# Attention over shared keys with the keys on the partitions, in a one-core graph-transformer kernel

## The chip, the core and the metric

The kernel runs on one core of a Trainium2 chip. The metric is the device time of one execution in microseconds; the median of several executions stands for a kernel. A profile of one further execution gives busy times, waits and the order of the work.

## The reference

The program is two layers of a graph network with 625 nodes of 1024 features. Each layer adds a graph convolution, a linear attention and a feed-forward part to its input. The change is inside the feed-forward part of the second layer, which itself begins with a softmax attention of four heads of 256 features. All heads share one set of keys and values:

```python
nx = _rmsnorm(X, g1)
Q = (nx @ Wq.T).reshape(B, S, H, dk).transpose(0, 2, 1, 3)   # 4 heads of 256
Kc = nx @ Wkc.T                                              # 625 x 256, one for all heads
Vc = nx @ Wvc.T
scores = jnp.einsum('bhsd,btd->bhst', Q, Kc) * scale         # scale = 1/16
attn = jax.nn.softmax(scores, axis=-1)
out = jnp.einsum('bhst,btd->bhsd', attn, Vc)
out = out.transpose(0, 2, 1, 3).reshape(B, S, d) @ Wo.T
X = X + out
```

Behind it come a shared expert and two of eight routed experts for each row. The weights that make Q and Kc are normal with a deviation of 0.02; everything is float32.

## The kernel before

The 625 nodes are five tiles of 125 (`NT`, `P`), padded to 626 columns where they lie in the free dimension (`NP`), which are two halves of 313 (`HN`)[...]. Up to the expert blocks the order on every engine is written by hand: `do(prep, pe, after, after2)` issues a piece of TensorE work (`pe`), issues its `after` just ahead of the next piece's `pe`, and its `after2` just ahead of the one after that. So what an engine does is in the order of the `do` calls, and an engine works strictly in that order; semaphores hold an instruction until its inputs are there and its output's buffer is free.

All double PSUM tiles (`ps2`, two banks) come from one set of three buffers, used in turn; single ones (`ps1`) from two. SBUF tiles come from pools with tags: `big` has two buffers of eight rows of 640 floats per partition, `w` six of one megabyte for weights.

In the attention, `nxT` holds the normalised rows with features on partitions. From it come the keys `kcT` (features on partitions, 2 x 626), the values `vc` (nodes on partitions) and, head by head, the queries `qT` (features on partitions, two buffers). The stage's loop over heads takes, per tile `t` of 125 queries:

- `score` (L1208): scores with queries on the partitions and 626 keys in the free dimension; then on VectorE the largest score of a row (L1219, L1220), on ScalarE the exponential with that as a bias and with the row's sum (L1223), and on VectorE the sum's reciprocal and the division of the row (L1228 to L1230);
- `turn_scores`: the five 125 x 125 transposes of the row block on TensorE (L1239), copied by VectorE and ScalarE (L1243, L1244) into `pT`, which has the keys on partitions;
- `attend`: for each half of a head's 256 features, the product of values and `pT` over the five key tiles, copied into `aT`.

The loop puts the next head's queries (`ahead`, in halves) and the last head's two `attend`s between the scores, so that TensorE has work while a row block is made. Behind the loop stand the loads of Wo, the last `attend`s, and `project(t)`, the product with Wo (tile `pX`), whose `prep` scales the residual on VectorE.

The program contains the whole computation twice. `attempt(False)` runs the first graph attention without subtracting a row's largest score and tests whether its denominators stayed in a range; two columns of ones and zeros (`inside`) are summed over the partitions by a product with ones in `ranks`, turned into the number `again`, and read by the engines at the end. If `again` is above zero, `attempt(True)` computes everything anew with the shift. In both, the attention described here subtracts the maximum.

Of the kernel before, what the change touches and what calls it, by code (L numbers as in the profile page):

```python
# [8 lines left out]
FP = mybir.dt.float32  # L9
# [3 lines left out]
AF = mybir.ActivationFunctionType  # L13
ALU = mybir.AluOpType
AX = mybir.AxisListType
# [3 lines left out]
N = 625  # L19
NT = 5  # L20
P = 125
NP = 626
HN = 313
# [5 lines left out]
D = 1024  # L29
KC = D // 128  # L30
NE = 8
NB = 17
NB_MIN = 10
FAR = -1.0e30
LIMIT = 60.0
LEAST, MOST = 1.0e-22, 1.0e25
# [13 lines left out]
def attempt(ctx: ExitStack, tc: tile.TileContext, w: dict, out: bass.AP, shifted: bool):  # L50

    nc = tc.nc

    const = ctx.enter_context(tc.tile_pool(name="const", bufs=1))
# [4 lines left out]
    def ps1(name):  # L59
        pool, n = psums[-1]  # L60
        return pool.tile([128, 512], FP, tag="ps1", name=name, bufs=n)

    def ps2(name):
        return psums[-1][0].tile([128, 2, 512], FP, tag="ps2", name=name, bufs=3)


    ident = const.tile([128, 128], FP, name="ident")
# [5 lines left out]
    ones = const.tile([128, 128], FP, name="ones")  # L73
# [3 lines left out]
    nc.vector.memset(blockmask[0:64, 0:64], 1.0)  # L77
    nc.vector.memset(blockmask[64:128, 64:128], 1.0)

    inside = const.tile([128, 2], FP, name="inside")  # L80
    nc.vector.memset(inside, 1.0)

    def test(col, src, n, pool):
# [11 lines left out]
    def copy(dst, src):  # L95

        turn[0] ^= 1
        if turn[0]:
            nc.vector.tensor_copy(dst, src)
        else:  # L100
            nc.scalar.activation(dst, src, AF.Copy)  # L101
# [21 lines left out]
    def group(dst, pairs):  # L123

        for i, (lhsT, rhs) in enumerate(pairs):
            nc.tensor.matmul(dst, lhsT=lhsT, rhs=rhs, start=(i == 0), stop=(i == len(pairs) - 1))  # L126

    def feat(name, pairs):

        p = ps2(name)  # L130
        for h in range(2):
            group(p[:, h, :HN], [(a, b[:, h * HN:(h + 1) * HN]) for a, b in pairs])
        return p[:, :, :HN]

    def halves(ap):
        return ap.rearrange("p (h n) -> p h n", h=2)

    def nodes(t):
        return slice(t * P, (t + 1) * P)
# [54 lines left out]
    big = graph.enter_context(tc.tile_pool(name="big", bufs=2))  # L194
# [7 lines left out]
    do = Stream()  # L202
    hold = {}
# [7 lines left out]
    class LinearAttention:  # L211
# [82 lines left out]
        def query(self, m):  # L294
            if m % 4 == 0:
                self.wq = Half(wpool, w[self.names[0]], m // 4)
            wq = self.wq

            def pe():
                hold["pq"] = feat("pq", [(wq(k, m % 4 * 128, 128), self.xnT[:, k, :]) for k in range(KC)])  # L300

            def after():
                pq = hold["pq"]
                qe = mix.tile([128, NP], FP, tag="qe", name="qe", bufs=1)
                nc.scalar.activation(halves(qe), pq, AF.Exp, bias=self.bq[:, m:m + 1])
                qf = mix.tile([128, NP], FP, tag="qf", name="qf", bufs=2)
                nc.scalar.activation(halves(qf), pq, AF.Relu, bias=self.bq[:, m:m + 1])  # L307
                nc.vector.scalar_tensor_tensor(qf, qe, 1.0, qf, op0=ALU.min, op1=ALU.add)
                hold["qf", m] = qf

            do(None, pe, after)
            self.work(8.5)
# [18 lines left out]
    with ExitStack() as st0:  # L331
# [9 lines left out]
        with ExitStack() as edges:  # L341
            pool = edges.enter_context(tc.tile_pool(name="l0e", bufs=1))
# [33 lines left out]
            up = pool.tile([128, EN], FP, name="up")  # L376
# [161 lines left out]
            ring = big.tile([128, 10, 940], BF, tag="big", name="ring", padded_shape=[128, 10, 1024])  # L538
# [9 lines left out]
            def score(dst, m, n, p):  # L548

                nc.vector.scalar_tensor_tensor(m, m, 0.2, m, op0=ALU.mult, op1=ALU.max)  # L550
                nc.vector.tensor_tensor(m, m, att[0:p].unsqueeze(1).to_broadcast([p, n, 256]), op=ALU.mult)
                nc.vector.tensor_reduce(dst, m.rearrange("p t (h e) -> p t h e", h=4), AX.X, ALU.add)
                if not shifted:
                    nc.vector.tensor_scalar(dst, dst, LIMIT, None, op0=ALU.min)
                    nc.scalar.activation(dst, dst, AF.Exp)
# [478 lines left out]
    for k in range(KC):  # L1034
# [3 lines left out]
        def pe():  # L1038
            hold["pa"] = feat("pa", [(xnh[k // 4][:, s, k % 4 * 128:k % 4 * 128 + 128], CT[:, s, :])
                                     for s in range(NT)])  # L1040

        def after(k=k):
            copy(halves(meanT[k // 4][:, k % 4, :]), hold["pa"])
# [3 lines left out]
    for m in range(KC):  # L1047
# [3 lines left out]
        a = m % 4  # L1051
# [30 lines left out]
    pool = attn.enter_context(tc.tile_pool(name="attn", bufs=1, reuse_waits="tile"))  # L1082
# [119 lines left out]
        value(t)  # L1202

    aT = bigT("aT")
    pT = big.tile([128, NT, D], FP, tag="big", name="pT")[:P, :, 0:NP]
    nc.gpsimd.memset(pT[:, :, N:NP], 0.0)

    def score(head, t):  # L1208
        q = qT[head % 2]

        def pe():
            psc = hold["psc", t] = ps2("psc")
            for h in range(2):
                group(psc[:P, h, :HN], [(q[:, a, nodes(t)], kcT[:, a, h * HN:(h + 1) * HN]) for a in range(2)])

        def after():
            psc = hold.pop(("psc", t))[:P, :, :HN]
            mx = pool.tile([P, 1], FP, tag="mx", name="mx", bufs=2)
            nc.vector.tensor_reduce(mx, psc, AX.XY, ALU.max)  # L1219
            nc.vector.tensor_scalar(mx, mx, -1.0 / 16.0, None, op0=ALU.mult)  # L1220
            pr = pool.tile([P, NP], FP, tag="pr", name="pr", bufs=3)
            den = pool.tile([P, 1], FP, tag="den", name="den", bufs=3)
            nc.scalar.activation(halves(pr), psc, AF.Exp, bias=mx, scale=1.0 / 16.0, accum_out=den)  # L1223
            hold["pr", t] = pr, den

        def after2():
            pr, den = hold["pr", t]
            nc.vector.tensor_tensor(den, den, pr[:, N:NP], op=ALU.subtract)  # L1228
            nc.vector.reciprocal(den, den)
            nc.vector.tensor_scalar(pr, pr, den, None, op0=ALU.mult)  # L1230

        do(None, pe, after, after2)

    def turn_scores(t):
        def pe():
            pr, _ = hold.pop(("pr", t))
            pp = hold["pp"] = [ps1("ppT").rearrange("p (c n) -> p c n", c=4) for i in range(2)]
            for s in range(NT):
                nc.tensor.transpose(pp[s // 4][:P, s % 4, :P], pr[:, nodes(s)], ident[:P, :P])  # L1239

        def after():
            pp = hold["pp"]
            nc.vector.tensor_copy(pT[:, 0:4, nodes(t)], pp[0][:P, :, :P])  # L1243
            nc.scalar.activation(pT[:, 4, nodes(t)], pp[1][:P, 0, :P], AF.Copy)  # L1244

        do(None, pe, after)

    def attend(head, a):
        def pe():
            hold["po", a] = feat("po", [(vc[:, s, a * 128:(a + 1) * 128], pT[:, s, :]) for s in range(NT)])  # L1250

        do(None, pe, lambda: copy(halves(aT[:, 2 * head + a, :]), hold["po", a]))

    for head in range(4):
        ahead = [query(head + 1, a) for a in range(2)] if head < 3 else [lambda h: None] * 2
        score(head, 0)
        score(head, 1)
        if head:
            attend(head - 1, 0)
            attend(head - 1, 1)  # L1260
        turn_scores(0)
        score(head, 2)
        turn_scores(1)
        score(head, 3)
        ahead[0](0)
        ahead[0](1)
        turn_scores(2)
        score(head, 4)
        turn_scores(3)
        ahead[1](0)  # L1270
        ahead[1](1)
        turn_scores(4)
    wo = [Half(wpool, w["Wo"], c) for c in range(2)]
    attend(3, 0)
    attend(3, 1)

    attn.close()
    pool = ctx.enter_context(tc.tile_pool(name="exp", bufs=1, reuse_waits="tile"))
# [160 lines left out]
    def ranks():  # L1439
        hold["prt"] = ps1("prt")  # L1440
        group(hold["prt"][:P, 0:NT * NE], [(before, flat)])
        group(hold["prt"][:P, NT * NE:2 * NT * NE], [(ones[:P, :P], flat)])
        group(hold["prt"][:P, 2 * NT * NE:2 * NT * NE + 2], [(ones[:, :P], inside)])

    do(None, ranks)
    ptot = hold["prt"][:, NT * NE:2 * NT * NE]
# [24 lines left out]
    for i in range(2):  # L1471
# [22 lines left out]
    exp_f = pool.tile([P, NB], FP, name="exp_f")  # L1494
    nc.vector.tensor_reduce(exp_f, blk, AX.X, ALU.add)
    meta = pool.tile([P, NB + 2], I32, name="meta")
    outside = pool.tile([P, 1], FP, name="outside")
    nc.vector.tensor_scalar(outside, hold["prt"][:P, 2 * NT * NE:2 * NT * NE + 1], -1.0, 256.0,
                            op0=ALU.mult, op1=ALU.add)
    nc.vector.tensor_tensor(meta[:, NB + 1:NB + 2], outside, hold["prt"][:P, 2 * NT * NE + 1:2 * NT * NE + 2],  # L1500
                            op=ALU.subtract)
    nc.vector.tensor_scalar(meta[:, 0:NB], exp_f, float(NE - 1), None, op0=ALU.min)
    nc.vector.tensor_copy(meta[:, NB:NB + 1], ends[3][:, NE - 1:NE])
    hidden(3)
# [71 lines left out]
    rest(NB_MIN)  # L1576
    again = None
    if not shifted:
        again = nc.values_load(meta[0:1, NB + 1:NB + 2], min_val=0, max_val=256,
                               skip_runtime_bounds_check_because="256 less two sums of up to 128 ones and zeros")  # L1580


    with tc.manual_schedule(engines={mybir.EngineType.PE, mybir.EngineType.DVE, mybir.EngineType.Pool}):
# [121 lines left out]
```

## Time and profile before

| what | value |
|---|---|
| three executions, us | 2294.43, 2296.43, 2296.47 |
| median, us | 2296.43 |
| profiled execution, its own time, us | 2290.41 |
| its span from first to last instruction, us | 2288.7 |
| mean granted clock of TensorE | 0.978 |
| attention stage, us from the start | 1309.7 to 1464.8 |
| projection with Wo to the first hidden layer, us | 1464.8 to 1536.9 |
| expert blocks, us | 1684 to 2211 |

PE is TensorE's matmuls, PEld its weight loads, DVE VectorE, ACT ScalarE, POOL GpSimd, SPq the queue that issues most transfers. A line of the timeline gives the start and the length in microseconds, engine, source line, operation, output tile and input tiles, shapes and a count; in brackets stands the idle time before it and what ended it. Matmuls are pipelined: the length of one runs to its end, and what it costs in a row of them is the distance from start to start. L126 is the helper that issues most matmuls, so they are told apart by their output tiles: `psc` scores, `ppT` transposes, `po` values times weights, `pq` queries, `pX` the projection. A float32 matmul of the program shows as two in the trace, a transpose as one.

### The profile page before, as it was taken

What the parts mean: (1) busy time and instruction counts of PE and PEld (TensorE: products, weight loads), DVE (VectorE), ACT (ScalarE), POOL (GpSimd) and SP (SyncE); (2) the same over time, 40 slices, a digit from 0 to 9 for tenths busy, and PEclk for the clock granted to TensorE, in tenths of its full rate; (3) what the DMA queues carried; (4) which work ended last, traced back from release to release, by engine and by line L of the source; (5) the groups of instructions that cost most, each with busy time, mean ns of one, the idle gap of its engine ahead of it and who ended that gap; (6) DMA issues with size and microseconds to landing.
All of it is one profiled execution on the core that took longest, in us unless ns stands there. A gap on an engine that the chain in (4) does not pass through costs nothing. (4 is left out here: it accounts for less than half of the span.)

```text
span 2288.7 us, 17693 instructions
## 1 busy us (share of the span) xinstructions
PE 2170.3 (95%) x7018; PEld 1228.9 (54%) x7018; DVE 734.7 (32%) x1342; ACT 196.1 (9%) x363; POOL 346.0 (15%) x351
## 2 busy tenths in 40 slices
PE   8988888987899999999999999999999999999998
PEld 6655554444445767754444777556754444444443
DVE  5868668655422640000111133232111111111112
ACT  2000010012200100000000011110000000000000
POOL 1667766300000220010000000010000000000010
PEclk9998998989999999999999999999999999999999
DMA  9352252530122110233003111030269898898643
GB/s 302 96 174 63 68 186 79 133 105 1 37 83 74 46 46 0 74 138 110 0 0 118 57 38 37 10 109 1 92 249 338 318 332 305 303 332 319 254 149 94
DMA packets 145852, 301.66 MB, mean 132 GB/s; under 512 B 12370, under 2 KB 22436, under 8 KB 145754
## 3 DMA queue, kind: packets, MB, share of 16 engines
q1 hardware_dynamic: 123412, 243.18, 29.6%
q0 software_dynamic: 17664, 47.47, 7.0%
q10 hardware_dynamic: 4678, 9.72, 1.4%
q8 instruction: 59, 0.97, 0.2%
q14 instruction: 39, 0.32, 0.0%
HBM read 277.49 MB, written 22.84 MB: 131 GB/s over the span
## 5 line engine op out<-in xcount | busy, mean ns | idle before, releaser
L126 PE MATMUL pu<-w,xgT 128*128 128x512 f32 x768 | 333.9, 593 | 1.9 <-DVE xgT L1086 1.9
L126 PEld LDWEIGHTS pu<-w,xgT 128*128 128x128 f32 x768 | 144.0, 190 | 174.8 <-issue 172.0
L126 PE MATMUL pyb<-w,hb 128*128 128x512 f32 x384 | 174.3, 598 | 2.5 <-ACT yb L101 2.1
L126 PE MATMUL pq<-xnT,w 128*128 128x313 f32 x512 | 143.0, 439 | 15.1 <-ACT qf L307 11.6
L126 PE MATMUL pv<-w,xnT 128*125 128x512 f32 x320 | 143.4, 602 | 3.7 <-issue 3.7
L126 PE MATMUL pk<-w,xnT 128*125 128x512 f32 x320 | 141.4, 595 | 4.7 <-DVE x L888 4.7
L126 PE MATMUL p<-tT,w 128*128 128x313 f32 x512 | 136.3, 428 | 0.4 <-DVE tT L1086 0.4
L126 PEld LDWEIGHTS pq<-xnT,w 128*128 128x128 f32 x512 | 99.6, 196 | 56.9 <-ACT qf L307 13.5
L126 PEld LDWEIGHTS pyb<-w,hb 128*128 128x128 f32 x384 | 69.8, 189 | 90.9 <-issue 74.9
L1539 DVE TENSOR_TENSOR su<-pu,su 128x512 f32<-128x512 f32 x24 | 16.6, 691 | 314.6 <-ACT su L1538 314.6
L126 PEld LDWEIGHTS p<-tT,w 128*128 128x128 f32 x512 | 96.8, 190 | 37.9 <-issue 1.2
L126 PEld LDWEIGHTS pk<-w,xnT 128*125 128x125 f32 x320 | 59.7, 189 | 78.9 <-issue 72.2
L126 PEld LDWEIGHTS pv<-w,xnT 128*125 128x125 f32 x320 | 60.4, 191 | 76.7 <-issue 75.9
L582 POOL DMA_INDIRECT table<-es,at x79 | 85.9, 1088 | 59.9 <-issue 27.2
L1522 POOL DMA_INDIRECT xg<-rows_d,slots x12 | 11.4, 947 | 524.7 <-PE pxg L1529 449.0
L568 POOL DMA_INDIRECT ga<-xl_d,si x79 | 81.1, 1027 | 32.1 <-issue 29.1
L568 POOL DMA_INDIRECT gb<-xr_d,di x79 | 79.6, 1008 | 24.1 <-issue 23.5
L706 PE MATMUL px<-w,oT 128*125 128x512 f32 x160 | 76.7, 639 | 4.1 <-DVE oT L326 2.3
L126 PE MATMUL px<-w,hT 128*125 128x512 f32 x160 | 70.6, 594 | 0.0
L126 PE MATMUL px<-w,oT 128*125 128x512 f32 x160 | 70.3, 592 | 0.0
L126 PE MATMUL ph<-meanT,w 128*128 128x313 f32 x256 | 70.1, 426 | 0.0
L126 PE MATMUL ph<-xnT,w 128*128 128x313 f32 x256 | 70.0, 427 | 0.0
(352 smaller groups left out, 2550.9 us busy)
## 6 DMA issues: line engine op xcount, KB each, us to landing
w<-in_eW_dram SPq DMA_DIRECT2D x144, 1024.0 KB
w<-in_L_Wk_dram SPq DMA_DIRECT2D x8, 1024.0 KB
w<-in_L_Wv_dram SPq DMA_DIRECT2D x8, 1024.0 KB
w<-in_L_Wq_dram SPq DMA_DIRECT2D x8, 1024.0 KB
w<-in_L_Wo_dram SPq DMA_DIRECT2D x8, 1024.0 KB
w<-in_W_self_dram SPq DMA_DIRECT2D x8, 1024.0 KB
w<-in_W_neigh_dram SPq DMA_DIRECT2D x8, 1024.0 KB
w<-in_sW_dram SPq DMA_DIRECT2D x8, 1024.0 KB
```

The source lines that it names most:

```text
L126: nc.tensor.matmul(dst, lhsT=lhsT, rhs=rhs, start=(i == 0), stop=(i == len(pairs) - 1))
L568: nc.gpsimd.indirect_dma_start(out=dst[0:p, j, :], out_offset=None, in_=src[:, :], in_offset=bass.IndirectOffsetOnAxis(ap=ix[0:p, lo + j:l ...
L582: nc.gpsimd.indirect_dma_start(out=table[:, :], out_offset=bass.IndirectOffsetOnAxis(ap=at[0:p, lo + j:lo + j + 1], axis=0), in_=es[0:p, l ...
L706: nc.tensor.matmul(hold["px", t][:P, c, :], lhsT=oT[:, k, nodes(t)], rhs=wo[c](k), start=(k == 0), stop=False)
L1522: nc.gpsimd.indirect_dma_start(out=xg, out_offset=None, in_=rows_d[:, :], in_offset=bass.IndirectOffsetOnAxis(ap=slots[:, b:b + 1], axis=0))
L1539: nc.vector.tensor_tensor(su, pu[:, 0, :], su, op=ALU.mult)
```

## The change

In `attempt(False)` the attention is a new function; the old one is kept, word for word, as `shifted_attention` for `attempt(True)`.

- The scores are made with the keys on the partitions: `kcT` is now the stationary and the query the moving operand. A tile `s` is 125 keys by 626 queries.
- No maximum is taken. VectorE copies the scores from PSUM with a minimum against 16 x 60, straight into one of eight slots of `ring` (in the buffer of tag `big` that `pT` had), and ScalarE takes the exponential in place. The slot is the moving operand of the values' product as it stands, so the transposes and their copies go.
- The denominators: VectorE adds a head's five tiles, a product with a matrix of ones sums over the partitions and lays the sums of all queries on all 128 partitions, and VectorE takes the reciprocal of 128 x 626.
- `attend` no longer copies its result; VectorE multiplies it by the reciprocals on its way from PSUM to `aT` (`divide`).
- One row of each head's reciprocals is kept by ScalarE (`recs`) and tested at the end against a range, into a third column of `inside`; `again` counts from 384 in place of 256.
- The order in the loop: the last head's denominators stand behind the first score of a head, and its two `attend`s behind the second and third. The last head's stand behind the loop: `attend`, denominators, `attend`, both divisions. The loads of Wo are called behind them.

```diff
+    def attention():
+        ring = big.tile([128, 8, 640], FP, tag="big", name="ring")
+        recs = pool.tile([128, NP], FP, tag="pr", name="recs", bufs=3)
+        nc.gpsimd.memset(recs, 1.0)
+
+        def pT(head, s):
+            return ring[:P, (NT * head + s) % 8, 0:NP]
+
+        def score(head, s):
+            q = qT[head % 2]
+
+            def pe():
+                psc = hold["psc", s] = ps2("psc")
+                for h in range(2):
+                    group(psc[:P, h, :HN], [(kcT[:, a, nodes(s)], q[:, a, h * HN:(h + 1) * HN]) for a in range(2)])
+
+            def after():
+                p = pT(head, s)
+                nc.vector.tensor_scalar(halves(p), hold.pop(("psc", s))[:P, :, :HN], 16.0 * LIMIT, None, op0=ALU.min)
+                nc.scalar.activation(p, p, AF.Exp, scale=1.0 / 16.0)
+
+            def after2():
+                if s == 1:
+                    hold["den", head] = pool.tile([P, NP], FP, tag="xs", name="den", bufs=2, padded_shape=[P, D])
+                    nc.vector.tensor_tensor(hold["den", head], pT(head, 0), pT(head, 1), op=ALU.add)
+                elif s:
+                    nc.vector.tensor_tensor(hold["den", head], hold["den", head], pT(head, s), op=ALU.add)
+
+            do(None, pe, after, after2)
+
+        def denominators(head):
+            def pe():
+                hold["pden"] = feat("pden", [(ones[:P, :], hold.pop(("den", head)))])
+
+            def after():
+                rec = hold["rec"] = pool.tile([128, NP], FP, tag="pr", name="rec", bufs=3)
+                nc.vector.reciprocal(halves(rec), hold["pden"])
+                nc.scalar.activation(recs[32 * head:32 * head + 1, :], rec[0:1, :], AF.Copy)
+
+            do(None, pe, after)
+
+        def attend(head, a):
+            do(None, lambda: hold.update({("po", a): feat("po", [(vc[:, s, a * 128:(a + 1) * 128], pT(head, s))
+                                                                 for s in range(NT)])}),
+               None if head == 3 else lambda: divide(head, a))
+
+        def divide(head, a):
+            nc.vector.tensor_tensor(halves(aT[:, 2 * head + a, :]), hold["po", a], halves(hold["rec"]), op=ALU.mult)
+
+        for head in range(4):
+            ahead = [query(head + 1, a) for a in range(2)] if head < 3 else [lambda h: None] * 2
+            score(head, 0)
+            if head:
+                denominators(head - 1)
+            score(head, 1)
+            if head:
+                attend(head - 1, 0)
+            score(head, 2)
+            if head:
+                attend(head - 1, 1)
+            score(head, 3)
+            ahead[0](0)
+            ahead[0](1)
+            score(head, 4)
+            ahead[1](0)
+            ahead[1](1)
+        do()
+        attend(3, 0)
+        denominators(3)
+        attend(3, 1)
+        for a in range(2):
+            divide(3, a)
+
+        c = pool.tile([128, NP], FP, tag="pr", name="c", bufs=3)
+        nc.vector.tensor_scalar(c, recs, 1.0 / MOST, 1.0 / LEAST, op0=ALU.max, op1=ALU.min)
+        nc.vector.tensor_tensor(c, c, recs, op=ALU.is_equal)
+        nc.vector.tensor_reduce(inside[:, 2:3], c, AX.X, ALU.min)
+
+    (shifted_attention if shifted else attention)()
     wo = [Half(wpool, w["Wo"], c) for c in range(2)]
-    attend(3, 0)
-    attend(3, 1)
...
-        group(hold["prt"][:P, 2 * NT * NE:2 * NT * NE + 2], [(ones[:, :P], inside)])
+        group(hold["prt"][:P, 2 * NT * NE:2 * NT * NE + 3], [(ones[:, :P], inside)])
...
-    outside = pool.tile([P, 1], FP, name="outside")
-    nc.vector.tensor_scalar(outside, hold["prt"][:P, 2 * NT * NE:2 * NT * NE + 1], -1.0, 256.0,
-                            op0=ALU.mult, op1=ALU.add)
-    nc.vector.tensor_tensor(meta[:, NB + 1:NB + 2], outside, hold["prt"][:P, 2 * NT * NE + 1:2 * NT * NE + 2],
-                            op=ALU.subtract)
+    within = pool.tile([P, 1], FP, name="within")
+    nc.vector.tensor_reduce(within, hold["prt"][:P, 2 * NT * NE:2 * NT * NE + 3], AX.X, ALU.add)
+    nc.vector.tensor_scalar(meta[:, NB + 1:NB + 2], within, -1.0, 384.0, op0=ALU.mult, op1=ALU.add)
```

More of the change, by code (lines that the diff above doesn't have):

```diff
@@ L78, in attempt @@
     nc.vector.memset(blockmask[64:128, 64:128], 1.0)
-    inside = const.tile([128, 2], FP, name="inside")
+    inside = const.tile([128, 3], FP, name="inside")
     nc.vector.memset(inside, 1.0)
@@ L1204, in attempt @@
     aT = bigT("aT")
[L1205 to L1272, printed above, removed]
+    def shifted_attention():
+        pT = big.tile([128, NT, D], FP, tag="big", name="pT")[:P, :, 0:NP]
+        nc.gpsimd.memset(pT[:, :, N:NP], 0.0)
+        def score(head, t):
+            q = qT[head % 2]
+            def pe():
+                psc = hold["psc", t] = ps2("psc")
+                for h in range(2):
+                    group(psc[:P, h, :HN], [(q[:, a, nodes(t)], kcT[:, a, h * HN:(h + 1) * HN]) for a in range(2)])
+            def after():
+                psc = hold.pop(("psc", t))[:P, :, :HN]
+                mx = pool.tile([P, 1], FP, tag="mx", name="mx", bufs=2)
+                nc.vector.tensor_reduce(mx, psc, AX.XY, ALU.max)
+                nc.vector.tensor_scalar(mx, mx, -1.0 / 16.0, None, op0=ALU.mult)
+                pr = pool.tile([P, NP], FP, tag="pr", name="pr", bufs=3)
+                den = pool.tile([P, 1], FP, tag="den", name="den", bufs=3)
+                nc.scalar.activation(halves(pr), psc, AF.Exp, bias=mx, scale=1.0 / 16.0, accum_out=den)
+                hold["pr", t] = pr, den
+            def after2():
+                pr, den = hold["pr", t]
+                nc.vector.tensor_tensor(den, den, pr[:, N:NP], op=ALU.subtract)
+                nc.vector.reciprocal(den, den)
+                nc.vector.tensor_scalar(pr, pr, den, None, op0=ALU.mult)
+            do(None, pe, after, after2)
+        def turn_scores(t):
+            def pe():
+                pr, _ = hold.pop(("pr", t))
+                pp = hold["pp"] = [ps1("ppT").rearrange("p (c n) -> p c n", c=4) for i in range(2)]
+                for s in range(NT):
+                    nc.tensor.transpose(pp[s // 4][:P, s % 4, :P], pr[:, nodes(s)], ident[:P, :P])
+            def after():
+                pp = hold["pp"]
+                nc.vector.tensor_copy(pT[:, 0:4, nodes(t)], pp[0][:P, :, :P])
+                nc.scalar.activation(pT[:, 4, nodes(t)], pp[1][:P, 0, :P], AF.Copy)
+            do(None, pe, after)
+        def attend(head, a):
+            def pe():
+                hold["po", a] = feat("po", [(vc[:, s, a * 128:(a + 1) * 128], pT[:, s, :]) for s in range(NT)])
+            do(None, pe, lambda: copy(halves(aT[:, 2 * head + a, :]), hold["po", a]))
+        for head in range(4):
[5 more added lines that the diff above has]
+                attend(head - 1, 1)
+            turn_scores(0)
+            score(head, 2)
+            turn_scores(1)
+            score(head, 3)
+            ahead[0](0)
+            ahead[0](1)
+            turn_scores(2)
+            score(head, 4)
+            turn_scores(3)
+            ahead[1](0)
+            ahead[1](1)
+            turn_scores(4)
+        attend(3, 0)
+        attend(3, 1)
@@ new lines, in attention, with pe, after, after2 @@
+    def attention():
[5 more added lines that the diff above has]
+        def score(head, s):
+            q = qT[head % 2]
+            def pe():
+                psc = hold["psc", s] = ps2("psc")
+                for h in range(2):
+                    group(psc[:P, h, :HN], [(kcT[:, a, nodes(s)], q[:, a, h * HN:(h + 1) * HN]) for a in range(2)])
+            def after():
+                p = pT(head, s)
+                nc.vector.tensor_scalar(halves(p), hold.pop(("psc", s))[:P, :, :HN], 16.0 * LIMIT, None, op0=ALU.min)
+                nc.scalar.activation(p, p, AF.Exp, scale=1.0 / 16.0)
+            def after2():
+                if s == 1:
[3 more added lines that the diff above has]
+                    nc.vector.tensor_tensor(hold["den", head], hold["den", head], pT(head, s), op=ALU.add)
+            do(None, pe, after, after2)
+        def denominators(head):
+            def pe():
+                hold["pden"] = feat("pden", [(ones[:P, :], hold.pop(("den", head)))])
+            def after():
+                rec = hold["rec"] = pool.tile([128, NP], FP, tag="pr", name="rec", bufs=3)
+                nc.vector.reciprocal(halves(rec), hold["pden"])
+                nc.scalar.activation(recs[32 * head:32 * head + 1, :], rec[0:1, :], AF.Copy)
+            do(None, pe, after)
+        def attend(head, a):
+            do(None, lambda: hold.update({("po", a): feat("po", [(vc[:, s, a * 128:(a + 1) * 128], pT(head, s))
[3 more added lines that the diff above has]
+            nc.vector.tensor_tensor(halves(aT[:, 2 * head + a, :]), hold["po", a], halves(hold["rec"]), op=ALU.mult)
+        for head in range(4):
+            ahead = [query(head + 1, a) for a in range(2)] if head < 3 else [lambda h: None] * 2
+            score(head, 0)
+            if head:
+                denominators(head - 1)
+            score(head, 1)
+            if head:
+                attend(head - 1, 0)
+            score(head, 2)
+            if head:
+                attend(head - 1, 1)
+            score(head, 3)
+            ahead[0](0)
+            ahead[0](1)
+            score(head, 4)
+            ahead[1](0)
+            ahead[1](1)
+        do()
+        attend(3, 0)
+        denominators(3)
+        attend(3, 1)
+        for a in range(2):
[4 more added lines that the diff above has]
+        nc.vector.tensor_reduce(inside[:, 2:3], c, AX.X, ALU.min)
@@ L1578, in attempt @@
     if not shifted:
-        again = nc.values_load(meta[0:1, NB + 1:NB + 2], min_val=0, max_val=256,
-                               skip_runtime_bounds_check_because="256 less two sums of up to 128 ones and zeros")
+        again = nc.values_load(meta[0:1, NB + 1:NB + 2], min_val=0, max_val=384,
+                               skip_runtime_bounds_check_because="384 less three sums of up to 128 ones and zeros")
     with tc.manual_schedule(engines={mybir.EngineType.PE, mybir.EngineType.DVE, mybir.EngineType.Pool}):
```

## The prediction

> **What bounds the kernel now.** I read the page's first part, then the busy time by stage, then TensorE's timeline of the changed stage. TensorE is the bound overall, and the stage that the change rewrites can be cut out exactly: it runs from the first score matmul (1309.7 us) to the first matmul of the output projection (1464.8 us).
>
> ```profile
> PE 2170.3 (95%) x7018; PEld 1228.9 (54%) x7018; DVE 734.7 (32%) x1342; ACT 196.1 (9%) x363; POOL 346.0 (15%) x351
> ...
> 1309.70:1464.80 155.10, 149.26 (x614) 108.30 (x614) 53.82 (x128) 27.66 (x68) 0.00 (x0) 0.99 0.10 34
> ...
> 1684.00:2211.00 527.00, 521.70 (x1344) 236.15 (x1342) 65.80 (x97) 28.66 (x48) 9.37 (x10) 1.00 0.84 305
> ```
>
> Columns of the last two: stretch, its length, busy time of PE, PEld, DVE, ACT, POOL, granted clock, DMA share, GB/s. In the attention stage VectorE works 54 us of 155 and DMA a tenth. In the expert stage, behind it, TensorE is still busy 522 us of 527. No wait of TensorE for a transfer shows between 1464.8 us and the end, so microseconds taken from the attention should reach the end.
>
> TensorE's timeline in one inner head and at the two ends of the stage:
>
> ```profile
> 1316.41 0.78 PE L1239 MATMUL ppT<-ident,pr 125*125 125x125 f32 x5 [2.29 <-DVE pr L1230]
> ...
> 1346.99 10.70 PE L126 MATMUL po<-pT,kvc 125*128 125x313 f32 x40
> 1357.53 0.71 PE L1239 MATMUL ppT<-ident,pr 125*125 125x125 f32 x5
> 1358.07 2.27 PE L126 MATMUL psc<-kvc,qT 128*125 128x313 f32 x8
> 1360.18 0.71 PE L1239 MATMUL ppT<-ident,pr 125*125 125x125 f32 x5
> ...
> 1451.92 1.18 PE L1239 MATMUL ppT<-ident,pr 125*125 125x125 f32 x5 [2.58 <-DVE pr L1230]
> 1452.89 12.03 PE L126 MATMUL po<-pT,kvc 125*128 125x313 f32 x40
> 1464.76 15.62 PE L126 MATMUL pX<-w,aT 128*125 128x512 f32 x36
> ```
>
> Reading start to start: 8 score matmuls take 2.11 us and 40 value matmuls 10.54, so one of 313 columns costs 0.2635 us; five transposes cost 0.54. (A program's fp32 matmul is two in the trace.) One score tile is 8 of these, 2.11; one product with V (an `attend`) 20, 5.27; one query chunk 32, 8.43. The stage then is:
> - scores 160 x 0.2635 = 42.2; queries of heads 1 to 3, 192 x 0.2635 = 50.6; values 160 x 0.2635 = 42.2; 20 groups of transposes x 0.54 = 10.8. Sum 145.8.
> - It lasts 1464.76 - 1309.74 = 155.0, so 9.2 us are gaps and slow matmuls: 2.4 in front of the first transposes, 0.6 twice and 2.75 in front of the last head's, 0.4 of slower transposes, and 1.3 because the last head's value matmuls start slow; the rest is rounding and small gaps.
>
> **The change on TensorE.** Removed: the 100 transposes, 10.8 us. Added: the products with ones, four heads x 4 matmuls of 313 columns in the trace = 16 x 0.2635 = 4.2. Scores and values keep number and shape (only the scores' operands swap). Work: 145.8 - 10.8 + 4.2 = 139.2 us. Were there no gap, the gain would be 15.8. What remains is to walk the new waits.
>
> **The other engines' prices.** Each new tile has a minimum from PSUM (L441, 806 ns), an exponential (L1223, 782; L245 at 512 columns from SBUF is 630, so 0.63 to 0.78, I take 0.78), and an addition into the denominator (L1010, 802). Per head come a reciprocal of 626 columns and two divides (L326, 810).
>
> ```profile
> L325 DVE RECIPROCAL z<-z 128x626 f32<-128x626 f32 x16 | 65.1, 4066 | 0.6
> L326 DVE TENSOR_TENSOR oT<-po,z 128x626 f32<-128x626 f32 x16 | 13.0, 810 | 1.7
> L441 DVE TENSOR_SCALAR u<-pct 125x626 f32<-125x626 f32 x6 | 4.8, 806 | 0.1
> L1010 DVE TENSOR_TENSOR CT<-CT,dinv 125x626 f32<-125x626 f32 x4 | 3.2, 802 | 0.0
> L245 ACT ACTIVATE ke<-kb 125x512 f32<-125x512 f32 x20 | 12.6, 630 | 115.3 <-DVE kb L243 115.3
> ```
>
> VectorE's sum: 20 x 0.81 + 16 x 0.80 + 4 x 4.07 + 8 x 0.81 + copies 2.8 + range test about 2.2 = 57 us, against 54 now, in a stage of 140: no bound by volume. The handovers are 0.20 us from TensorE's last issue to VectorE, 0.1 between VectorE and ScalarE, 0.1 back to TensorE.
>
> **An inner head, from its first score at 0.**
> - Score 0 needs the second half of this head's queries after 0.53 us. Its copy starts 0.20 after the last query matmul and takes 0.81, so the matmul goes at 1.16: 0.6 us of stall, in three heads 1.9. Today a group of transposes (0.54) stands in front and the stall is 0.1. Score 0 ends at 2.7, the denominators' product at 3.8, score 1 at 5.9, the first `attend` at 11.2, score 2 at 13.3, the second `attend` at 18.5.
> - The reciprocal runs 4.0 to 8.0 on VectorE. Behind it wait score 1's minimum (to 8.9), its exponential and the addition; the one-row copy of the reciprocals is ahead of that exponential on ScalarE, done by 8.8, and delays nothing.
> - There are three double PSUM tiles. Score 2 needs the denominators' tile back at 11.2 (free at 8.0), the second `attend` needs score 1's at 13.3 (free at 8.9), score 3 the first `attend`'s at 18.5 (divided by 12.2). The eight-slot ring is never short: a slot is rewritten by score 3, after both `attend`s. No stall: 3 us of room.
>
> **Head 0.** Four scores run back to back: the minima end at 3.1, 5.2, 7.9, 10.5 (an addition that waits for an exponential holds the third and fourth), and the fourth score and the query need them at 6.3 and 8.4: first at 3.1, second at 5.2. No stall; the 2.4 us of today are gone. The table load of the exponential (1.28) lies in this slack.
>
> **The last head** has no queries to fill. Scores 3 and 4 end at 20.7 and 22.8; score 4's minimum is queued behind the addition for score 3, which waits for its exponential, so the last exponential ends at 25.2. The `attend` started at 22.8 needs it after 2.1 us: stall 0.4. It ends at 28.4, the denominators at 29.5, the last `attend` at 34.8. Reciprocal 29.7 to 33.8, divide to 34.6. The projection's first PSUM tile is the one that this divide frees: ready at 34.74, asked for at 34.78. So the reciprocal is just covered here, and each microsecond that it is longer is paid. The other divide (to 35.8) is needed only by the eighth pair of matmuls, some 6 us later. The test's three VectorE operations (2.2 us) stand ahead of the residual's scaling, which the projection wants 14 us later.
>
> Sum: 139.2 + 1.9 + 0.4 = 141.5 us, that is 13.5 less. On the other queues nothing moves: a 626-column clearing replaces the clearing of a pad on GpSimd, long before its use; the four loads of Wo stay in their place on SP. In the router the third column and the exchange of two small VectorE operations lie under hidden-layer matmuls.
>
> **Two rules against the rows.** The Trainium skill's "VectorE: DVE Perf Modes" (section "First, the fixed hardware budget") says that the reciprocal is an iterative divide with a repeat count of 8. At eight cycles an element and that page's 0.96 GHz I estimate 5.2 us; the row says 4.07. With 5.2 the inner heads still hold, the end pays 1.15: gain 12.4. I take the row; it reads SBUF where the new one reads PSUM, but L448 against L1010 (810 against 802) makes that small.
>
> "TensorE: Matmul & The Clock Gate" (Part 1) wants an idle window of about 3.4 us before the clock halves. Here 2.6 us were followed by half clock:
>
> ```profile
> 1451.90:1452.90 1.00, 0.97 (x6) 1.00 (x6) 0.46 (x1) 0.00 (x0) 0.00 (x0) 0.63 0.00 0
> 1452.90:1455.50 2.60, 2.60 (x6) 1.69 (x6) 1.40 (x2) 0.28 (x1) 0.00 (x0) 0.50 0.00 0
> ```
>
> By the row the gap costs 1.3 us and goes with it, since no new gap passes 0.7; by the rule the halving has another cause and may recur: gain 12.2.
>
> **Rivals.**
> 1. *As walked* (72%): 13.5 less, 2282.9; own range 2280 to 2286 for the prices above and the medians' spread of 2.
> 2. *The reciprocal becomes a wait* (13%). If from PSUM it takes twice as long, 8.1 us, score 2 waits 1.0 in three heads and the projection 4.0: gain 6.4, 2290.0. For it: VectorE is in order and it stands ahead of everything. Against it: 4066 ns in all 16 cases.
> 3. *The gain is swallowed behind the stage* (8%): expert weights arrive no earlier, 2293 to 2297. For it: DMA share 0.84 and 305 GB/s there. Against it: 12.6 MB per block in 43.5 us, while that queue peaks above 330 GB/s (38 us), and loads start when TensorE frees a buffer, so they move with it.
> 4. *Slower* (2%), by one thing: the range test. One false entry makes the kernel run the whole shifted attempt again: near 2 x 2290 = 4580. It decides when a denominator leaves 1e-22 to 1e25. Normalised rows through weights of 0.02 give queries and keys of deviation 0.64, scores of 16 x 0.41 / 16 = 0.41: denominators are near 680.
> 5. *Longer stalls than walked* (5%), for instance whole-ring waits: an `attend` that waits for score 1's exponential (9.7 instead of 5.9) costs 4 us in three heads, gain 1.5: no change; with a further 2 us per head it is slower. The waits that the built program carries name the head's own tiles, which speaks against it.
>
> **How the numbers follow.** The sum is made on the profiled execution, 2290.41 us (span 2288.7), 6 us under the median of 2296.43; I take it off the median: 2282.9. The range of 2278 to 2291 adds rival 2 and an upside of 2.3 (no stalls), and leaves out 3 to 5. A difference under 0.2% (4.6 us) is no change: the border is 2291.8. Faster holds 1, 2 and a part of 3: 0.90; same most of 3 and half of 5: 0.07; slower 0.03.
>
> **What would show it.** Right: no transposes between the scores; the stage 141 to 142 us; reciprocals of about 4.1 us; 0.6 us in front of three heads' first score; full clock at the last head; the stretch from the first projection matmul to the end unchanged at 824 us. Wrong: a wait of scores or `attend`s for a reciprocal, a projection waiting for a divide, half clock in the stage, or a transfer named in front of expert matmuls.

## The result

The changed kernel takes 2279.23 us (median of four, 2277.89 to 2281.07) where the kernel before takes 2295.43 (median of four, 2293.71 to 2296.47): ratio 0.9931, 95% interval 0.9914 to 0.9948. It is faster by 16.2 us; 13.5 were forecast, and the interval in microseconds is 12 to 20. The profiled execution took 2278.52, its span is 2276.8 us. The two profiled executions are only 11.9 us apart (2290.41 and 2278.52), because the changed kernel's stage begins 2.2 us later (1311.98 against 1309.74 us), behind work that the change hardly touches. So the change is read from the stage, and the whole time from medians.

The page's busy times of the changed kernel:

```profile
PE 2159.0 (95%) x6934; PEld 1219.1 (54%) x6934; DVE 737.9 (32%) x1269; ACT 189.2 (8%) x323; POOL 348.1 (15%) x351
```

The busy time by stage, of the attention and of everything behind it (stretch, length, busy time of PE, PEld, DVE, ACT and POOL, granted clock, DMA share, GB/s):

```profile
1311.90:1453.20 141.30, 140.18 (x531) 99.28 (x530) 53.27 (x51) 19.37 (x27) 0.00 (x0) 1.00 0.11 38
1453.20:2276.80 823.60, 809.42 (x2270) 401.94 (x2268) 134.58 (x227) 46.99 (x77) 38.23 (x37) 1.00 0.62 223
```

The whole kernel has lost 11.3 us of TensorE's busy time (2170.3 to 2159.0). TensorE now works through the stage at the full clock with 1.1 us of idle time. From its first score to the first projection matmul the stage takes 1453.19 - 1311.98 = 141.2 us; the forecast was 141.5. Before, it took 1464.76 - 1309.74 = 155.0, from this first score on:

```profile
1309.74 4.38 PE L126 MATMUL psc<-kvc,qT 128*125 128x313 f32 x16
```

What is behind the stage takes 823.6 us in place of 823.9 and has not changed.

TensorE's timeline of the changed kernel at the first score, in the first inner head and in the last head:

```profile
1311.98 8.59 PE L126 MATMUL psc<-qT,kvc 128*125 128x313 f32 x32
...
1339.38 0.69 PE L126 MATMUL psc<-qT,kvc 128*125 128x313 f32 x2
1340.45 1.85 PE L126 MATMUL psc<-qT,kvc 128*125 128x313 f32 x6 [0.38 <-DVE qT L99]
1342.13 1.22 PE L126 MATMUL pden<-den,ones 125*128 125x313 f32 x4
1343.19 2.27 PE L126 MATMUL psc<-qT,kvc 128*125 128x313 f32 x8
1345.30 5.43 PE L126 MATMUL po<-ring,kvc 125*128 125x313 f32 x20
1350.57 2.27 PE L126 MATMUL psc<-qT,kvc 128*125 128x313 f32 x8
...
1437.22 4.38 PE L126 MATMUL psc<-qT,kvc 128*125 128x313 f32 x16
1441.44 5.59 PE L126 MATMUL po<-ring,kvc 125*128 125x313 f32 x20
1446.87 1.22 PE L126 MATMUL pden<-den,ones 125*128 125x313 f32 x4
1447.92 5.43 PE L126 MATMUL po<-ring,kvc 125*128 125x313 f32 x20
1453.19 7.03 PE L126 MATMUL pX<-w,aT 128*125 128x512 f32 x16
```

The transposes are gone from between the scores. The only bracket is the wait for the copy of the queries' second half: the third matmul starts 1.07 us after the first where 0.53 would do. At the end, 5.59 us for 20 value matmuls in place of 5.43 is a wait of 0.16 us for the last exponential.

VectorE's groups in the stage of the changed kernel (instructions, busy time, mean ns, idle time before them):

```profile
L1315 DVE RECIPROCAL rec<-pden 128x626 f32<-128x626 f32 x4 | 16.3, 4071 | 4.5 <-PE pden L126 4.5
L1297 DVE TENSOR_SCALAR ring<-psc 125x626 f32<-125x626 f32 x20 | 16.0, 799 | 40.4 <-PE psc L126 40.4
L1305 DVE TENSOR_TENSOR den<-den,ring 125x626 f32<-125x626 f32 x12 | 9.7, 811 | 10.0 <-ACT ring L1298 10.0
L1326 DVE TENSOR_TENSOR aT<-po,rec 128x626 f32<-128x626 f32 x7 | 5.7, 810 | 11.2 <-PE po L126 11.1
```

The reciprocal from PSUM costs 4071 ns, about as from SBUF (4066). The other prices hold too, but for the exponential, which takes 725 ns where 782 were counted.

### The profile page after: what moved, and what is told of

It is laid out like the page before. It is cut to its first block, busy times and chain, and to the rows that moved or that the text cites. A ratio compares the mean times of both kernels' runs of the same rounds, so it can differ in the third digit from the quotient of the medians.

```text
span 2276.8 us, 17389 instructions
## 1 busy us (share of the span) xinstructions
PE 2159.0 (95%) x6934; PEld 1219.1 (54%) x6934; DVE 737.9 (32%) x1269; ACT 189.2 (8%) x323; POOL 348.1 (15%) x351
## 5 line engine op out<-in xcount | busy, mean ns | idle before, releaser
L126 PE MATMUL pq<-xnT,w 128*128 128x313 f32 x512 | 145.2, 444 | 15.3 <-ACT qf L307 10.5
L126 PE MATMUL pk<-w,xnT 128*125 128x512 f32 x320 | 141.0, 594 | 4.7 <-DVE x L888 4.7
L1620 DVE TENSOR_TENSOR su<-pu,su 128x512 f32<-128x512 f32 x24 | 16.6, 691 | 314.6 <-ACT su L1619 314.6
L1603 POOL DMA_INDIRECT xg<-rows_d,slots x12 | 11.3, 943 | 524.8 <-PE pxg L1610 449.0
```

Of the source, the lines that this page charges most:

```text
L1603: nc.gpsimd.indirect_dma_start(out=xg, out_offset=None, in_=rows_d[:, :], in_offset=bass.IndirectOffsetOnAxis(ap=slots[:, b:b + 1], axis=0))
L1620: nc.vector.tensor_tensor(su, pu[:, 0, :], su, op=ALU.mult)
```

## The experiments

Stage times are from the first score matmul to the first projection matmul in the run's profile. All three profiles of the changed kernel give 141.2, so a tenth of a microsecond counts here, while the whole time wanders by several.

**The transposes put back as idle work.**

```diff
                     group(psc[:P, h, :HN], [...])
+                pp = ps1("spare").rearrange("p (c n) -> p c n", c=4)
+                for i in range(NT):
+                    nc.tensor.transpose(pp[:P, i % 4, :P], ident[:P, :P], ident[:P, :P])
```

> The changed kernel with five 125 x 125 transposes behind every score tile, into a PSUM tile that nobody reads; nothing waits for them. If the gain is TensorE's own work, the stage from the first score to the first projection matmul goes from 141.2 us to 151.9 (20 x 0.54 = 10.8 more, less the 0.16 that they fill ahead of the last head's values) and the whole time rises by as much. If the gain was the latency of the softmax chain alone, idle time takes them up and the stage grows by less than 3.

Measured: stage 1464.58 - 1312.56 = 152.0 us, 823.4 behind it, whole time 2289.73 (one execution).

```profile
1312.56:1464.58 152.02, 150.90 (x630) 110.21 (x628) 53.55 (x51) 19.38 (x27) 0.00 (x0) 1.00 0.10 35
```

TensorE is busy 150.9 us, where the changed kernel's stage, cut at the same two matmuls, has 140.1; its idle time stays 1.1 us, and the stage is 10.8 us longer. So TensorE is full in this stage, and work taken from it there is time.

**One part of the change alone: no maximum, transposes kept**, in the kernel before. Its output is the same softmax without the shift.

```diff
-            nc.vector.tensor_reduce(mx, psc, AX.XY, ALU.max)
-            nc.vector.tensor_scalar(mx, mx, -1.0 / 16.0, None, op0=ALU.mult)
...
-            nc.scalar.activation(halves(pr), psc, AF.Exp, bias=mx, scale=1.0 / 16.0, accum_out=den)
+            nc.scalar.activation(halves(pr), psc, AF.Exp, scale=1.0 / 16.0, accum_out=den)
```

> The kernel before with one part of the change alone: no row maximum, the exponential taken straight from PSUM with no bias; the transposes stay. From the end of a score to its transposes the chain falls from 3.4 to 2.25 us (0.2 + 0.97 + 0.2 + 0.2 + 0.55 + 0.1). By my theory that leaves gaps of 0.15 us in head 0, 1.7 in front of the last transposes and 0.5 of small ones where there were 9.2, and full clock behind them: the stage is 148.3 us, so about half of the gain is this part and half the transposes. If the transposes are all of it, the stage stays within 1 us of 155.0.

Measured: stage 1457.35 - 1309.41 = 147.9 us. The end of its stage in TensorE's timeline, and the granted clock of the stretch behind the last gap:

```profile
1443.96 0.71 PE L1236 MATMUL ppT<-ident,pr 125*125 125x125 f32 x5
1446.11 0.87 PE L1236 MATMUL ppT<-ident,pr 125*125 125x125 f32 x5 [1.45 <-DVE pr L1227]
1446.81 10.70 PE L126 MATMUL po<-pT,kvc 125*128 125x313 f32 x40
1457.35 18.19 PE L126 MATMUL pX<-w,aT 128*125 128x512 f32 x42
```

```profile
1447.00:1450.00 3.00, 3.00 (x13) 2.12 (x13) 1.22 (x2) 0.28 (x1) 0.00 (x0) 1.00 0.00 0
```

With the maximum go 7.1 us of the 13.8: the gap in head 0 and the small ones, 1.1 us of the last one, and the half clock behind it, which 1.45 us of idle time did not bring. The other 6.7 us (147.9 to 141.2) are the transposes less the product with ones, 10.8 - 4.2 = 6.6, with the remaining gaps of either side nearly equal. The two halves of the gain have different causes, a chain's latency and TensorE's own work.

**The reciprocal issued twice.**

```diff
                 nc.vector.reciprocal(halves(rec), hold["pden"])
+                nc.vector.reciprocal(halves(rec), hold["pden"])
```

> The changed kernel with each head's reciprocal issued twice, so that it holds VectorE for 8.1 us in place of 4.07. By the walk of the queues (room of 3 us in the inner heads, none at the end): score 2 of heads 1 to 3 waits 1.1 us for the denominators' PSUM tile, 3.2 in all, and the projection waits 4.0 for the last head's divide; the stage goes to 148.4 us, to 149.7 if those 4 us halve the clock again as the gap of 2.6 did before. If VectorE has slack everywhere, it stays at 141.2; if it has none, 4 x 4.07 come on top: 157.5.

Measured: stage 1460.63 - 1312.56 = 148.1 us, and 825.5 behind it, 1.9 more. Its timeline in an inner head and at the end, and the clock behind the last gap:

```profile
1352.29 2.35 PE L126 MATMUL psc<-qT,kvc 128*125 128x313 f32 x8 [0.98 <-DVE rec L1316]
...
1452.15 5.43 PE L126 MATMUL po<-ring,kvc 125*128 125x313 f32 x20
...
1456.46 4.07 DVE L1316 RECIPROCAL rec<-pden 128x626 f32<-128x626 f32 x1
...
1460.56 1.53 DVE L1327 TENSOR_TENSOR aT<-po,rec 128x626 f32<-128x626 f32 x2
1460.63 3.56 PE L126 MATMUL pX<-w,aT 128*125 128x512 f32 x4 [3.05 <-issue]
```

```profile
1460.60:1463.00 2.40, 2.37 (x3) 1.16 (x4) 2.37 (x4) 0.68 (x1) 0.00 (x0) 0.50 0.03 7
```

Score 2 of heads 1 to 3 waits for the second reciprocal, to be read in the bracket, and starts 1.14 us late, as walked. The end differs from the walk: the projection starts at 1460.63, just behind the reciprocal (1460.53), while the first divide is still running. The matmuls that read the two divides' results come later, and their waits are covered. So the projection's PSUM tile is the one that the reciprocal frees, not the one that the divide frees; the wait that the built program carries on that matmul names the reciprocal too. The wait is then 3.2 us in place of 4.0, and in the changed kernel itself the end has about 0.9 us of room (1452.19 + 0.1 against 1453.19) where I had found none. Half clock follows the 3.05 us of idle time, and the 1.9 us more behind the stage are the projection's start at that clock.

**The range test left out**: no clearing and copies of the row, no test; the kernel would not notice a denominator out of range.

```diff
-                nc.scalar.activation(recs[32 * head:32 * head + 1, :], rec[0:1, :], AF.Copy)
...
-        nc.vector.tensor_scalar(c, recs, 1.0 / MOST, 1.0 / LEAST, op0=ALU.max, op1=ALU.min)
-        nc.vector.tensor_tensor(c, c, recs, op=ALU.is_equal)
-        nc.vector.tensor_reduce(inside[:, 2:3], c, AX.X, ALU.min)
```

> The changed kernel without the range test of the denominators: no clearing and no copies of one row of the reciprocals, no three VectorE operations at the end (the third column keeps its ones). All of it lies under other work by the walk: stage 141.2 us, no change within 0.1. If the test's operations delay the exponentials on ScalarE or the projection, the stage is 0.5 to 3 us shorter.

Measured: stage 1453.95 - 1312.74 = 141.2 us and 823.9 behind it: the test is free.

**The minimum left out**, so that large scores would overflow:

```diff
-                nc.vector.tensor_scalar(halves(p), hold.pop(("psc", s))[:P, :, :HN], 16.0 * LIMIT, None, op0=ALU.min)
-                nc.scalar.activation(p, p, AF.Exp, scale=1.0 / 16.0)
+                nc.scalar.activation(halves(p), hold.pop(("psc", s))[:P, :, :HN], AF.Exp, scale=1.0 / 16.0)
```

> The changed kernel without the minimum against 16 x 60: ScalarE takes the exponential straight from PSUM into the ring, so VectorE has 20 operations of 0.81 us less. By my theory VectorE's volume is not on the path: only the last head's 0.16 goes, stage 141.0 us. If the chain minimum, exponential, addition still holds TensorE anywhere else, the stage falls by 1 us or more.

Measured: stage 1500.10 - 1359.06 = 141.0 us. Taking 20 x 0.8 us from VectorE is worth 0.16 us, the last head's stall: VectorE's volume is not on the path.

**The remaining stalls taken out.**

```diff
-                for h in range(2):
-                    group(psc[:P, h, :HN], [(kcT[:, a, nodes(s)], q[:, a, h * HN:(h + 1) * HN]) for a in range(2)])
+                for a in range(2):
+                    for h in range(2):
+                        nc.tensor.matmul(psc[:P, h, :HN], lhsT=kcT[:, a, nodes(s)],
+                                         rhs=q[:, a, h * HN:(h + 1) * HN], start=(a == 0), stop=(a == 1))
...
-                elif s:
-                    nc.vector.tensor_tensor(hold["den", head], hold["den", head], pT(head, s), op=ALU.add)
+                elif s and (head, s) != (3, 3):
+                    for i in (3, 4) if (head, s) == (3, 4) else (s,):
+                        nc.vector.tensor_tensor(hold["den", head], hold["den", head], pT(head, i), op=ALU.add)
```

> The changed kernel with two edits against its remaining stalls: each score tile takes the first half of the features for both column halves before the second (1.05 us of cover for the copy of the queries' second half, needed at 1.07), and in the last head the addition for tile 3 is issued behind the minimum of tile 4. By the walk the stalls of 0.54 in three heads fall to 0.02 and the 0.16 of the last head goes: stage 139.5 us in place of 141.2, whole time 1.7 us less, at the edge of what the medians can tell. If those stalls are not the copy's but a fixed cost of a head's change, the stage stays at 141.2.

Measured: stage 1502.68 - 1363.12 = 139.6 us. The first score of a head and the last head's values no longer wait:

```profile
1390.55 2.38 PE L1294 MATMUL psc<-qT,kvc 128*125 128x313 f32 x8
1392.77 1.22 PE L126 MATMUL pden<-den,ones 125*128 125x313 f32 x4
...
1491.09 5.43 PE L126 MATMUL po<-ring,kvc 125*128 125x313 f32 x20
```

The first score takes 2.22 us from start to start where it took 2.75. The whole time does not show it: 2324.78 us (eight executions) beside 2323.85 for the changed kernel on the same chip, with executions 15 us apart and more. It was measured again:

> The kernel with fewer stalls once more: stage 139.6 us, and a median 1.6 us under that of the changed kernel beside it if the medians can tell that much; the ratio to the kernel before 0.0007 lower.

Stage 1503.54 - 1363.99 = 139.6 us again; median 2324.03 of nine executions (ratio to the kernel before 0.9931, 0.9902 to 0.9960), beside 2322.61 for the changed kernel. The stage is shorter by 1.6 us, shown twice; that the whole is faster than the changed kernel is not shown.

**The changed kernel and the kernel before, repeated.** The first medians are 16.2 us apart and the stages 13.8.

> The changed kernel once more, with more executions against the kernel before. The stage's profile gives 13.8 us and the rest of the program runs the same code, so by my theory the medians differ by 13.8 (12.5 to 15), ratio 0.9940. If something outside the stage became faster as well, the 16.2 of the first medians return: ratio 0.9930 or less.

> The changed kernel a third time, beside the kernel before against itself. If only the stage counts: 13.8 us less, ratio 0.9940 on a chip of about 2295 us. If the stretch before the stage is faster as well in most executions (not in the one profiled), 16 or more: ratio 0.9930.

> The kernel before against itself. It shows what the comparison calls a difference when there is none: ratio 1.000 within 0.002, the stage 155.0 us, and 824 us behind it. If its own ratio strays by 0.1% or more, the 2.4 us by which the medians of the change exceed the stage's 13.8 are no finding.

Measured: 0.9928 (0.9904 to 0.9952) and 0.9929 (0.9912 to 0.9947) for the change; 1.0004 (0.9981 to 1.0026) for the kernel before against itself. On the chips of these two sets every kernel took some 45 us longer, all of it ahead of the attention stage (which starts at 1357 to 1365 us there). The medians differ by 16.6 and 18.1 us, the means by 17.4 and 15.7. The last of these, 2339.9 - 2324.2 over 38 and 22 executions, has an interval of 12 to 19, which takes in 13.8; in the first comparison the means differ by 15.9. The stage of the changed kernel is 141.2 us in both repeats (1497.85 - 1356.65 and 1501.14 - 1359.94), but that of the kernel before is not 155.0: it is 1521.47 - 1364.97 = 156.5.

```profile
1371.64 0.78 PE L1239 MATMUL ppT<-ident,pr 125*125 125x125 f32 x5 [2.29 <-DVE pr L1230]
1372.25 3.72 PE L126 MATMUL psc<-kvc,qT 128*125 128x313 f32 x8
...
1508.54 0.86 PE L1239 MATMUL ppT<-ident,pr 125*125 125x125 f32 x5 [2.58 <-DVE pr L1230]
1509.24 12.39 PE L126 MATMUL po<-pT,kvc 125*128 125x313 f32 x40
```

Here the gap of 2.3 us in head 0 was followed by half clock as well (the eight score matmuls take 3.52 us from start to start and not 2.11), and in the first profile it was not. The clock records of the traces point to why. In each of the twelve, all changes of the granted clock lie multiples of 3.413 us apart, so the clock goes by steps of that length. The gap in head 0, by these steps, in the first profile and in this one, and the step behind the last gap in this one:

```profile
1312.21:1315.62 3.41, 1.91 (x8) 1.03 (x6) 1.06 (x4) 2.15 (x3) 0.00 (x0) 1.00 0.64 248
1315.62:1319.04 3.42, 2.63 (x13) 1.96 (x13) 2.28 (x8) 1.04 (x3) 0.00 (x0) 1.00 0.02 5
```

```profile
1369.50:1372.92 3.42, 1.28 (x8) 1.16 (x9) 1.74 (x5) 1.44 (x4) 0.00 (x0) 1.00 0.03 10
1372.92:1376.33 3.41, 3.41 (x10) 2.28 (x9) 1.77 (x5) 0.61 (x3) 0.00 (x0) 0.50 0.02 5
...
1509.45:1512.86 3.41, 3.41 (x8) 2.18 (x7) 1.20 (x2) 0.27 (x1) 0.00 (x0) 0.50 0.00 0
```

In the first profile the gap lies across a border of two steps, in which TensorE was busy 56% and 77%, and full clock followed. In this one 2.1 us of it lie in one step, busy 38%, and the next step ran at half clock. The other gaps of the stage fit: half clock followed steps that were 24% and 27% busy (the last gap in the two profiles) and 15% (the doubled reciprocal), and not one of 68% (no maximum). Where between 38% and 56% the border lies, these steps do not show.

The same kernel's stage thus has two lengths, 155.0 and 156.5, by where its gaps fall, and the changed one's only one. The stages of this pair of profiles are 15.3 us apart. How often each happens was not measured. The start of the stage wanders too: in the first comparison and the first four experiments the changed kernel and its variants began it 2 to 3 us later than the kernels with the old attention, here it began it 5.0 us earlier than the kernel before (1359.94 against 1364.97). So what part of the 15.7 to 18.1 us between means and medians is the stage's second length stays open; what is left over is within the comparison's own uncertainty.

## Why the prediction was right

- *TensorE is the bound and the gain reaches the end*: shown. Work put back costs its full time (152.0 us), and the part behind the stage is 823.4 to 823.9 us in every profile whose projection starts at full clock. Rival 3, a gain swallowed by the expert weights, falls. (Its range, 2293 to 2297, lay wholly above the border of 2291.8, so *faster* should have had 0.85 and not 0.90.)
- *TensorE's work, 145.8 to 139.2 us*: shown by its two ends, 10.8 us of transposes put back, and 6.7 us between the kernel without maximum and the changed one.
- *The gaps of 9.2 us*: shown. 7.1 of them go with the maximum alone. Their size rests on one profile, and that is its weakness: the half clock was charged once, for the last gap, and in the repeat it comes in head 0 too, which makes the stage 1.5 us longer. That moves the forecast from 13.5 to as much as 15, toward the measured 16.2. That the profile in hand had the shorter stage was chance, as far as these traces show.
- *The stall for the queries' copy*, 0.63 forecast in each of three heads: the score is 0.64 longer (2.75 us against 2.11), but the wait itself is 0.54, since the matmul starts 0.06 us behind the copy's end (1339.58 + 0.81 against 1340.45) and not 0.15; the six matmuls behind it take 0.1 us more than their price. That it is the copy's wait is shown by the reordering, which takes away 0.53.
- *The reciprocal has 3 us of room in the inner heads*: shown by doubling it; score 2 waits 1.14 us. Rival 2 put about the right price on a doubled reciprocal in the inner heads (1.0), but the reciprocal does not take longer from PSUM: it is 4071 ns, and the 5.2 us estimated from the repeat count in "VectorE: DVE Perf Modes" (section "First, the fixed hardware budget") do not occur.
- *At the end each microsecond more is paid*: wrong. The projection's tile comes free with the reciprocal, not with the divide, and 0.9 us of room is left, so 4.07 us more cost 3.2. I had counted the three buffers strictly in turn. The result did not depend on it.
- *The last head's stall* of 0.4 us is 0.16. The last exponential ends 24.9 us behind the head's first score and not 25.2; its chain holds two exponentials of 725 ns where 782 were counted, which is 0.1 us, and the rest is handovers shorter than counted.
- *Full clock in the new stage*: shown, 1.00 in its stretch, with no stall over 0.54 us. The alternative that I drew from "TensorE: Matmul & The Clock Gate" (Part 1), that the halving has another cause than the gap and recurs, falls: it went with the gap in the kernel without maximum, and came back with a 3.05 us one when the reciprocal was doubled. The page's figure of about 3.4 us for the idle window is more than the idle time that was enough here, 2.3 to 2.6 us; what the traces show at 3.41 us is the step, and a step need not be wholly idle.
- *The range test is free and in range*: shown, 141.2 us without it; rival 4 did not happen. Rival 5's whole-ring waits do not exist: the first value matmul after score 1 starts 2.11 us behind it (1345.30), while the reciprocal (to 1347.46) still holds that score's minimum.

## What to carry to other kernels

Cut out the stage, price TensorE's instructions by their start-to-start distance, and what is left of the stage's length is waits; then walk each new wait through the queues by hand. A latency chain (maximum, exponential, normalisation, transpose) costs only where no other TensorE work stands between its links, here in the first and last head, and there half clock behind a gap can add another half to the bill (1.5 us to a gap of 2.3). One profile may show the cheap case of such a gap. Where a buffer is reused, ask which instruction releases it in the built program; counting buffers in turn is not enough.

## What was not expected of the hardware

Half clock behind a gap is not a matter of the gap's length alone. In this stage it came after 2.3 us of idle time in one profile of two, after 2.6 and 3.05 us in three of three, and after 1.45 us and less it did not; what agreed with it each time is how much of the gap fell into one step of 3.413 us. Elsewhere in the program a gap of 2.0 us was enough (819.87 to 821.86 us with the doubled reciprocal), and one of 3.5 us was not (279.37 to 282.86 us in the kernel without the maximum).

The same program took some 45 us longer on other chips, all of it ahead of the attention stage; the changed kernel's stage was alike to a tenth, and what follows it to half a microsecond. The cause was not sought.
